# Background work at the joint of two graph-attention layers: read-ahead of second-level sums, late maxima and shifts rearranged

## The chip, the cores and the metric

The kernel runs on one core of one Trainium2 chip. The metric is device time in microseconds (us); lower is better. The core has TensorE (PE in the profile; its weight loads are PEld), VectorE (DVE), ScalarE (ACT), GpSimd (POOL), and 16 DMA engines, whose transfers are issued here from two queues: SyncE's (SP) and POOL's.

## The reference

A graph of N = 2708 nodes with 1024 features goes through two attention layers; `adj` is its 0/1 adjacency matrix. Each layer adds its output to its input.

```python
# layer 0
h = jnp.maximum(_layernorm(x), 0.0)
f = h @ Wf + bf; g = h @ Wg + bg
scores = jnp.where(adj > 0, relu(f @ g.T), NEG)
x = x + softmax(scores, axis=1) @ (h @ W + bW)
# layer 1
h0 = jnp.maximum(_layernorm(x), 0.0)
h = h0 @ W1
e = leaky_relu(h @ a1 + (h @ a2).T, 0.2)
scores = jnp.where(adj > 0, e, NEG)
x = x + relu(softmax(scores, axis=1) @ h)
```

In layer 1 the scores depend on two numbers for each node only, so that its attention weights are made on DVE and ACT. The row maximum that the softmax subtracts follows from the largest second number among a node's neighbours; the code calls these the maxima.

## The kernel before, in words

**Tiles and panels.** The nodes are cut into 22 row tiles: 20 full ones of 128, which go two and two into ten pairs, and two for what is left over (`MONO`, `TINY`). The outputs are made panel by panel: five panels, whose widths are 576, 576, 532, 512 and 512 nodes. The weights of a panel lie transposed: 22 tiles `S[t]`, rows the neighbours, columns the panel's nodes.

**Products.** All large products are in fp32 and use Winograd's form of Strassen's scheme: seven products of half size (M1 to M7) with sums of operands before them and sums of results after them. `aggregate` (L885) makes the features of a panel, normalized h times weights; `project` (L1202) multiplies them by the layer's W. `aggregate` takes its products in the order M1, M5, M2, M6, M3, M7, M4; each runs over ten pairs of tiles and four banks of PSUM (80 matmuls). Product M7 has a point in its middle, after the sixth pair, at which the corner of the left-over tiles is added (`into_m15`, with `gw` banks). In layer 1 panel 0 uses `aggregate`; panels 1 to 4 use `aggregate_quartered` (L1039), in which each of the seven products is cut into seven again. That wants second-level sums of h.

**Second-level sums.** `put_quarters(m, k)` (L392) makes one: it reads the two halves of product m's operand for quad k (two pairs, which are panel k's rows in layer 0) from `hr_d`, does four additions of 128x256 on DVE (tile name `hq`) and stores two halves to `hs2_d`. Reads and stores go through POOL's queue. There are 7 x 5 = 35, seven for each panel, and seven can be made as soon as layer 0 has done that panel's rows.

**Background work.** Work that no product waits for at once is put in lists with a declared cost: `put(us, go, fetch, ..., to)` (L198) appends to `later` (the ordinary list) or to `lazy`. `one` (L201) first issues the reads (`fetch`) of the next `ahead[0]` entries, then does the first entry. `behind(us)` (L211), called at fixed places among the matmuls, grants a credit, and entries of `later` are written out until it is used up; with `spare[0]` set and `later` empty it goes on with `lazy`. `flush` (L218) empties `later`; `exps_until` and `quarters_until` (L416) force what a product needs. `from_slots[0]` decides whether an `hq` tile is taken from the common slots (54 tiles of 128x576) or from the 12 stream buffers. These lists set the order in which the instructions are written; the framework takes that order as a priority and fills idle engines with what is ready, except where `nc.hold` keeps one engine's order.

**Layer 0 to layer 1.** For each panel p layer 0 runs `scores`, the projection of queries for the next panel or, for the last, the projection of panel 3 (L1678 to L1681), and `aggregate`. Panel 4's rows are then projected by pairs of tiles (`by_pair=True`, `rate=0.0`). As row tiles become final, `rows_done` (L1520) adds moments, normalization and dot products to `later`, then the maxima that the new rows bring to panels (`put_max`, L1346: two entries for each panel and pair, one load of a mask through SP and one DVE operation `raise_max`), and second-level sums to `lazy`. For panel 4's two pairs (8 and 9) this is the branch at L1535. Layer 1 has for each panel `shifts1` (L1502: five small transposes of the panel's maxima `mx` on PE, `mx_ps`, L849, and small DVE operations) and `weights1` (L1705: two spreads by PE, L253, then 22 tiles: one ACT operation, two DVE operations, an exponential, and an addition to the running sum `sm`). `take_shifts(p)` (L1781) flushes `later` first. For panel 1 both are hooked into panel 0's aggregate: shifts after M6, weights after M3 (L1794).

```python
        spare[0], from_slots[0] = 0 < p < NP - 1, p == NP - 1        # layer 0, L1688
        G[p] = aggregate(0, p, S, got["sm"], then)
        spare[0] = False
```

So seven sums each of panels 0, 1 and 2 are made in the next panel's aggregate of layer 0, and the fourteen of panels 3 and 4 in layer 1's first one, where `ahead[0]` is 2.

Of the kernel before, what the change touches and what calls it, by code (L numbers as in the profile page):

```python
# [57 lines left out]
def kernel(  # L58
# [26 lines left out]
    NP = N // W  # L85
# [112 lines left out]
    def put(us, go, fetch=None, takes_psum=False, ready=None, to=later):  # L198
        to.append([us, fetch, go, takes_psum, ready])

    def one(of=None):  # L201
        of = later if of is None else of
        for it in of[:ahead[0]]:
            if it[1]:
                it[1]()
                it[1] = None
        us, _, go = of.pop(0)[:3]
        go()
        return us
# [179 lines left out]
    BY_QUARTERS = (M1, M5, M2, M6, M7, M3, M4)  # L389
    made_quarters = {}  # L390

    def put_quarters(m, k):  # L392

        two = []

        def fetch():
            if from_slots[0]:
                two.extend(slot(f"hq{h}", (P, 2, WH)) for h in range(2))
            else:
                t = stream("hq", (P, 4, WH))  # L400
                two.extend(t[:, 2 * h:2 * h + 2] for h in range(2))
            for h in range(2):
                nc.gpsimd.dma_start(two[h], hr_d[:, m, h, :, k])

        def go():
            a11, a12, a21, a22 = (two[h][:, i] for h in range(2) for i in range(2))
            add(a22, a21, a22)
            sub(a21, a11, a21)
            sub(a11, a22, a11)
            sub(a12, a12, a11)  # L410
            for h in range(2):
                store(hs2_d[:, m, 2 * h:2 * h + 2, k], two[h])
            made_quarters[m] = made_quarters.get(m, 0) + 1
        put(1.7, go, fetch, to=lazy)

    def quarters_until(m):  # L416
        while made_quarters.get(m, 0) < NK:
            one(lazy)

    u = consts.tile([P, NC], FP, name="u")  # L420
    v = consts.tile([P, NC], FP, name="v")
# [412 lines left out]
    def load_mask(p, q, k):  # L834
        mt = slot("maskl", (P, WX), BF)
        w = width[p]
        load(mt[:, :w], mk_d[p][:, q, k, :])
        return mt
# [46 lines left out]
    def aggregate(l, p, S, sm, then={}, rate=3.0):  # L885
# [35 lines left out]
        def left_over(ps, e, s, start=False):  # L921


            two = stream("hl", (P, W + 2 * P))
            load(two, hgl_d[l][:, e])
            for d in range(NH):
                nc.tensor.matmul(ps[d], two[:, d * P:(d + 1) * P], S[MONO][:, s], start=start, stop=False,
                                 skip_group_check=True)
            for d in range(NH):
                g = slice(B32 * d, B32 * d + NY)  # L930
                nc.tensor.matmul(ps[d], two[g, W + d % 2 * P:W + (d % 2 + 1) * P], S[TINY][g, s], start=False, stop=start, skip_group_check=True)
# [43 lines left out]
        def scale():  # L975
            for e, s, k in ((0, slice(0, w), w), (1, hi, h)):
# [2 lines left out]
        accumulate(left, right, NQ, h, order, then, evict, "g",  # L979
                   {**prepare, M3: lambda: inverse.append(inverse_sums(p, sm)), M7: scale}, rate=rate,  # L980
                   by_k=True, more={M2: lambda ps: left_over(ps, 0, lo), M3: lambda ps: left_over(ps, 0, hi),
                                    M4: lambda ps: left_over(ps, 1, lo), (M7, NQ // 2): into_m15})
        nc.vector.tensor_tensor(of(1, lo), of(1, lo), by(lo, h), OP.mult)
        return [t.rearrange("p (c i) -> p c i", c=NH) for t in G]

# [357 lines left out]
        t = units[q][k]  # L1343
        nc.vector.scalar_tensor_tensor(mx[p][:n, :w], mk[:n], f[1][:n, t:t + 1], mx[p][:n, :w], op0=OP.add, op1=OP.max)

    def put_max(p, q):  # L1346
        for k in range(2):
            mk = []
            put(0.7, lambda k=k, mk=mk: raise_max(p, q, k, mk[0][:, :width[p]]),
                lambda k=k, mk=mk: mk.append(load_mask(p, q, k)))  # L1350

    def scores(p, B):

# [166 lines left out]
    def rows_done(t, xt):  # L1520

        done_rows[t] = xt

        def dots(k):
            c = t if k else col_of[t]
            dot(f[k][:, c:c + 1], done_rows[t], halves(wab[k]))
            if k == 1:
                nc.vector.tensor_scalar(f2s[:, t:t + 1], f[1][:, t:t + 1], ALPHA, None, op0=OP.mult)
            elif t == MONO:
                nc.gpsimd.dma_start(f[0][:NM, HALF:HALF + 1], f[0][NM:, c:c + 1])  # L1530

        q, k = pair_of.get(t, (LEFT, t - MONO))
        mine = units[q]
        whole = all(s in done_rows for s in mine)
        if panel_of[t] == NP - 1:  # L1535
            done_rows[t] = row_halves("h_last")
            normalize(xt, done_rows[t])
            if whole and q == NQ - 1:
                tc.keep_in_program_order(nc.scalar.activation(stats.tile([P, 1], FP, name="warm"), eps, AF.Exp))
            raise_it = lambda: raise_max(0, q, k, first_mask[t][:, :width[0]])  # L1540
            if not whole:
                dots(1)
                raise_later.append(raise_it)
                put(1.6, lambda: dots(0))
            else:
                raise_later.pop()()
                dots(1)
                raise_it()
                put(1.6, lambda: dots(0))
                rest = []  # L1550
                make = lambda: rest.append(pair_h(q, *(done_rows[s] for s in pairs[q])))
                if q == NQ - 1:
                    got["zm"] = shifts1(0, make)
                else:
                    make()
                rest[0]()
                for p in range(1, NP):
                    put_max(p, q)
                if q == NQ - 1:
                    for m in BY_QUARTERS:  # L1560
                        put_quarters(m, q // 2)
            return

        def met():
            known.add(q)
            for p in range(NP):
                if generated[p] > q:
                    put_max(p, q)
        put(1.5, lambda: moments(xt))
        put(0.5, lambda: normalize(xt))  # L1570
        put(1.6, lambda: dots(0))
        put(1.6, lambda: dots(1))
        if whole and q == LEFT:
            put(0.0, lambda: left_h(1, *(done_rows[s] for s in mine)))
            put(0.0, met)
        elif whole:
            put(2.7, lambda: pair_h(q, *(done_rows[s] for s in pairs[q])))
            put(0.0, met)
            quads_met[q // 2] = quads_met.get(q // 2, 0) + 1
            if quads_met[q // 2] == 2:  # L1580
                put(0.0, lambda: [put_quarters(m, q // 2) for m in BY_QUARTERS])
# [84 lines left out]
    for p in range(NP):  # L1666
        got["S"], got["acc"] = scores(p, B)
        generated[p] = NQ + 1
        ahead[0] = 2
        S = got["S"]  # L1670
        hooks = {M1: lambda p=p: take_max(p), M2: lambda p=p: take_softmax(p)}
        if p == 0:
            hooks[M1] = lambda: (take_max(0), sums_until(3))
            sums_h()
        if p + 1 < NP:
            B = project_q(p + 1, hooks)
        else:
            nc.hold = ("vector",)  # L1678
            project(0, p - 1, G.pop(p - 1), finish0(p - 1), hooks)
            nc.hold = ()  # L1680
            scores_before()  # L1681
        then = {M4: lambda: sums_until(NQ), M5: prepare_W} if p == 0 else {}
        ahead[0] = 1 if p == 0 else 2
        if p == NP - 2:
            then[M2] = lambda: first_masks(NP - 1, 0)
            then[M6] = lambda: first_masks(NP - 1, 1)
            then[M7] = lambda: first_masks(NP - 1, 2)
        spare[0], from_slots[0] = 0 < p < NP - 1, p == NP - 1  # L1688
        G[p] = aggregate(0, p, S, got["sm"], then)
        spare[0] = False  # L1690
        if p == 0:
            flush()
            ahead[0] = 2
            for s in range(1, NP):
                columns_to_row(r_d[s], s, r_[:, first_col[s]:])
            spread_wa()
        if p < NP - 2:
            project(0, p, G.pop(p), finish0(p), {M1: lambda p=p: first_masks(p + 1, 0),
                                                 M5: lambda p=p: first_masks(p + 1, 1),
                                                 M7: lambda p=p: first_masks(p + 1, 2)})  # L1700
# [79 lines left out]

    def take_shifts(p):  # L1781
        flush()
        got["zm"] = shifts1(p)

    def take_weights(p):
# [4 lines left out]
    for p in range(NP):  # L1790
        S, sm = got["P"]
        then = {}
        if p + 1 < NP:
            then = dict(zip((M2, M6) if p else (M6, M3), (lambda p=p: take_shifts(p + 1), lambda p=p: take_weights(p + 1))))  # L1794
        spare[0] = p == 0
        g = aggregate_quartered(p, S, sm, next_right, then, fine=1.0) if p else aggregate(1, p, S, sm, then, rate=4.0)
        hooks = {}
        if p + 1 < NP:
            next_right = quarters_of(p + 1, got["P"][0])
            hooks = {M7: next_right["first"]}  # L1800
        project(1, p, g, finish1(p), hooks, by_pair=(p == NP - 1), rate=1.7)
# [29 lines left out]
```

## Time and profile before

| | us |
|---|---|
| median of 8 runs | 3108.97 (3105.69 to 3111.55) |
| profiled execution, device time | 3109.62 |
| its span | 3107.8 |
| busy in the span: PE, PEld | 3003.0, 2301.9 |
| busy in the span: DVE, POOL, ACT | 2067.8, 505.2, 463.5 |
| mean granted PE clock | 0.986 of full speed |

The joint in PE's timeline (us from the span's start):

| stage | from, to |
|---|---|
| layer 0, aggregate of panel 4 | 1948 to 2080 |
| layer 0, projection of panel 4 by pairs | 2080 to 2129 |
| layer 1, shifts and first weights of panel 0 | 2129 to 2147 |
| layer 1, aggregate of panel 0 | 2147 to 2323 |
| layer 1, projection of panel 0 | 2323 to 2372 |
| layer 1, panel 1 | from 2372 |

How to read it: lines of DVE and ACT carry L45, because a wrapper issues them; operations are told apart by the names of their tiles. `out<-in` names what is written and read, `x14` the count of neighbouring like instructions. In a list of waits the columns are the waiting instruction, what released it, the total, how often and the longest. The device time lies 1.8 us above the span, since it counts what stands around it.

### The profile page before, as it was taken

How to read it: one execution, taken by the hardware profiler on the slowest of the kernel's cores; microseconds unless marked ns; L12 is line 12 of the kernel's file. 1: busy time of each engine (PE TensorE's matmuls, PEld its weight loads, DVE VectorE, ACT ScalarE, POOL GpSimd, SP SyncE). 2: the span in 40 equal slices, each digit the busy share in tenths (PEclk: the TensorE clock that was granted, in tenths of full speed). 3: DMA queues.
4: the chain of work that ended last, by engine and by line, in shares of the span. 5: the costliest groups of instructions: out<-in, count | busy, mean ns of one | idle time of the engine just before them, and what ended most of it. 6: DMA issues, size and time to landing. Idle time of an engine off the chain costs nothing.

```text
span 3107.8 us, 41683 instructions
## 1 busy us (share of the span) xinstructions
PE 3003.0 (97%) x14630; PEld 2301.9 (74%) x14630; DVE 2067.8 (67%) x4615; ACT 463.5 (15%) x817; POOL 505.2 (16%) x786
## 2 busy tenths in 40 slices
PE   8998999899999999999999999998979999999998
PEld 4576777657877588885888886875757969879694
DVE  5776692776751686616974377658787767887853
ACT  3420020000200101101020002203131121312200
POOL 1421101310112110223111101111322011020202
PEclk9999999999999999999999999998989999999999
DMA  6989967998566796668957577587877768878786
GB/s 224 298 256 268 300 245 257 301 277 230 165 239 155 224 251 221 243 157 251 282 189 250 170 219 239 204 278 276 263 235 254 273 197 299 282 271 293 267 294 246
DMA packets 448577, 764.70 MB, mean 246 GB/s; under 512 B 175776, under 2 KB 262592, under 8 KB 448368
## 3 DMA queue, kind: packets, MB, share of 16 engines
q1 hardware_dynamic: 393008, 598.31, 61.1%
q0 software_dynamic: 55360, 163.73, 16.2%
q8 instruction: 116, 1.90, 0.2%
q14 instruction: 93, 0.76, 0.1%
HBM read 627.95 MB, written 133.91 MB: 245 GB/s over the span
## 4 chain that ended last, share of the span: by engine, by line
PE 72%; issue 9%; DVE 9%; DMA 6%; POOL 2%; SPq 2%; ACT 1%; POOLq 0%; DVEq 0%; ACTq 0%
PE sz L1377 6%; PE gx L661 6%; PE gy L661 5%; PE gz L1066 5%; PE gz L661 5%; PE sx L1377 4%; PE pz L1266 4%; PE sy L1377 4%; PE px L1266 4%; PE py L1266 3%; PE gx L1066 3%; PE gy L1066 3%; PE M_ps L574 3%; PE qz L661 3%; PE gv L661 2%
## 5 line engine op out<-in xcount | busy, mean ns | idle before, releaser
L1377 PE MATMUL sz<-B,As 128*128 128x288 f32 (+2 forms) x1200 | 293.6, 394 | 9.5 <-DVE st L45 8.8
L1377 PEld LDWEIGHTS sz<-B,As 128*128 128x128 f32 x1200 | 228.4, 191 | 59.8 <-DVE st L45 12.9
L1377 PE MATMUL sx<-B,As 128*128 128x288 f32 (+2 forms) x800 | 202.1, 396 | 12.8 <-DMA As<-hs_d 11.3
L1377 PE MATMUL sy<-B,As 128*128 128x288 f32 (+2 forms) x800 | 199.0, 392 | 0.0
L661 PE MATMUL gz<-Sa,hc 128*128 128x288 f32 (+2 forms) x800 | 188.3, 396 | 5.8 <-DMA hc<-hg_d 5.8
L1377 PEld LDWEIGHTS sx<-B,As 128*128 128x128 f32 x800 | 152.7, 192 | 46.8 <-DMA As<-hs_d 9.0
L661 PEld LDWEIGHTS gz<-Sa,hc 128*128 128x128 f32 x800 | 153.3, 192 | 39.1 <-DMA hc<-hg_d 6.3
L1377 PEld LDWEIGHTS sy<-B,As 128*128 128x128 f32 x800 | 151.7, 190 | 30.6 <-DVE st L45 0.3
L1066 PE MATMUL gz<-quarter,hc 128*128 128x128 f32 (+2 forms) x1344 | 168.8, 279 | 3.8 <-DVE gT L45 3.7
L143 POOL DMA_DIRECT2D out_dram<-x_res x180 | 88.8, 500 | 479.0 <-DVE x_res L45 472.7
L1066 PEld LDWEIGHTS gz<-quarter,hc 128*128 128x128 f32 x1344 | 160.6, 191 | 5.1 <-DVE gT L45 4.5
L1266 PE MATMUL pz<-w,ps 128*128 128x512 f32 x320 | 142.1, 594 | 0.8 <-DVE pt L45 0.8
L1266 PE MATMUL py<-w,ps 128*128 128x512 f32 x320 | 141.9, 593 | 0.0
L1266 PE MATMUL px<-w,gT 128*128 128x512 f32 x320 | 141.2, 593 | 0.6 <-issue 0.6
L143 POOL DMA_DIRECT2D mk_d<-mask x55 | 35.8, 651 | 531.4 <-DVE mask L45 524.7
L1266 PEld LDWEIGHTS pz<-w,ps 128*128 128x128 f32 x320 | 60.2, 190 | 77.1 <-issue 71.0
L1266 PEld LDWEIGHTS py<-w,ps 128*128 128x128 f32 x320 | 60.6, 190 | 75.5 <-issue 73.1
L574 PE MATMUL M_ps<-wgT,wfT 128*128 128x512 f32 x256 | 112.6, 596 | 1.6 <-ACT hsT L45 1.6
L1266 PEld LDWEIGHTS px<-w,gT 128*128 128x128 f32 x320 | 60.1, 190 | 72.0 <-issue 69.2
L661 PE MATMUL gy<-T,hc 128*128 128x288 f32 (+2 forms) x480 | 111.6, 394 | 0.0
L661 PEld LDWEIGHTS gy<-T,hc 128*128 128x128 f32 x480 | 91.2, 190 | 19.5
L977 POOL TENSOR_TENSOR gT<-gT,rr 128x2304 f32<-128x2304 f32 (+5 forms) x12 | 44.4, 3702 | 372.4 <-issue 158.0
(377 smaller groups left out, 5806.5 us busy)
## 6 DMA issues: line engine op xcount, KB each, us to landing
hc<-hg_d SPq DMA_DIRECT2D x175, 512.0 KB
As<-hs_d SPq DMA_DIRECT2D x150, 512.0 KB
hc<-hr_d SPq DMA_DIRECT2D x119, 512.0 KB
hc<-hs_d SPq DMA_DIRECT2D x112, 512.0 KB
w<-wt_d SPq DMA_DIRECT2D x96, 512.0 KB
w<-in_L_gnn_W_dram SPq DMA_DIRECT2D x72, 512.0 KB
md<-md_d SPq DMA_DIRECT2D x56, 512.0 KB
adj_i<-in_adj_dram SPq DMA_DIRECT2D x200, 128.0 KB
```

The costliest lines, as they stand in the source:

```text
L143: nc.gpsimd.dma_start(a, b)
L574: nc.tensor.matmul(ps, wfT[a][c // NH][:, c % NH, :], wgT[b][c], start=(c == 0), stop=(c == NC - 1))
L661: nc.tensor.matmul(ps[d], left(m, k, d), right(m, k), start=(start and k == 0), stop=(k == K - 1), skip_group_check=True)
L977: nc.gpsimd.tensor_tensor(of(e, s), of(e, s), by(s, k), OP.mult)
L1066: nc.tensor.matmul(ps[:, d], lhs[:, d * P:(d + 1) * P], inner_right(m, n, k), start=(start and k == 0 and d == 0), stop=(k == NK - 1), ski ...
L1266: nc.tensor.matmul(ps, left[i][m][:, k, :], w_[k], start=(start and k == 0), stop=(k == NH - 1), skip_group_check=True)
L1377: nc.tensor.matmul(ps[:n, :h], lefts[q][:, i % 2, c, :n], B[m][c // 2][:, c % 2, :h], start=(start and c == 0), stop=(c == NH - 1), skip_g ...
```

## The change

It has six parts.

1. Entries of `lazy` are read four ahead once `from_slots` is set, and so are those of `later` in layer 1's first aggregate (`ahead[0]` 4 instead of 2; back to 2 after it).
2. The seven sums of panel 4's rows go to `later` instead of `lazy`.
3. Of the maxima that pairs 8 and 9 bring, those of panel 1 stay in `later`; those of panels 2 to 4 go to `lazy`, after the sums. Shifts of panels from 2 on first empty `lazy`.
4. `spare` is also set in layer 0's last aggregate, so that panel 3's seven sums can be made there, and in panel 1 of layer 1.
5. In layer 1's first aggregate the shifts of panel 1 move from behind M6 to behind M3, and its weights from behind M3 into the middle of M7, after the corner.
6. `quarters_until` falls back on `later` when `lazy` is empty.

```diff
     def one(of=None):
         of = later if of is None else of
-        for it in of[:ahead[0]]:
+        for it in of[:4 if of is lazy and from_slots[0] else ahead[0]]:
...
-    def put_quarters(m, k):
+    def put_quarters(m, k, to=lazy):
...
-        put(1.7, go, fetch, to=lazy)
+        put(1.7, go, fetch, to=to)
 
     def quarters_until(m):
         while made_quarters.get(m, 0) < NK:
-            one(lazy)
+            one(lazy if lazy else later)
...
-                                    M4: lambda ps: left_over(ps, 1, lo), (M7, NQ // 2): into_m15})
+                                    M4: lambda ps: left_over(ps, 1, lo),
+                                    (M7, NQ // 2): lambda: (into_m15(), then.get((M7, "middle"), lambda: None)())})
...
-    def put_max(p, q):
+    def put_max(p, q, to=later):
...
-                lambda k=k, mk=mk: mk.append(load_mask(p, q, k)))
+                lambda k=k, mk=mk: mk.append(load_mask(p, q, k)), to=to)
...
-                for p in range(1, NP):
-                    put_max(p, q)
+                put_max(1, q)
                 if q == NQ - 1:
                     for m in BY_QUARTERS:
-                        put_quarters(m, q // 2)
+                        put_quarters(m, q // 2, later)
+                    for p in range(2, NP):
+                        for s in (NQ - 2, NQ - 1):
+                            put_max(p, s, lazy)
...
-        spare[0], from_slots[0] = 0 < p < NP - 1, p == NP - 1
+        spare[0], from_slots[0] = p > 0, p == NP - 1
...
     def take_shifts(p):
         flush()
+        while p > 1 and lazy:
+            one(lazy)
         got["zm"] = shifts1(p)
...
-            then = dict(zip((M2, M6) if p else (M6, M3), (lambda p=p: take_shifts(p + 1), lambda p=p: take_weights(p + 1))))
-        spare[0] = p == 0
+            then = dict(zip((M2, M6) if p else (M3, (M7, "middle")), (lambda p=p: take_shifts(p + 1), lambda p=p: take_weights(p + 1))))
+        spare[0] = p < 2
+        ahead[0] = 2 if p else 4
```

## The prediction

> **What bounds the kernel now.** First the busy times of the page: TensorE (PE) works 3003.0 of 3107.8 us, so only its 105 idle us and its slow-clock time can be won. Then its waits in the stretch that the change touches (1940 to 2520 us): three of its four largest stalls there stand before the maxima of layer 1 (`mx_ps`, L849) and their spreading (L253).
>
> ```profile
> PE mx_ps L849 <- DVE gT L45: 18.8, 1, 18.8
> PE mx_ps L849 <- DVE mx L45: 8.3, 1, 8.3
> PE sp_ps L253 <- DVE m L45: 3.9, 1, 3.9
> PE gv L661 <- DVE m L45: 1.4, 1, 1.4
> ```
>
> PE's timeline places the 18.8: inside product M3 (`gy`) of layer 1's first aggregate. Columns: start, duration, instructions, idle time before and its releaser.
>
> ```profile
> 2229.83 15.68 PE L661 MATMUL gy<-P,hc 128*128 128x288 f32 x64
> ...
> 2248.08 2.21 PE L661 MATMUL gy<-P,hc 128*128 128x288 f32 x8
> 2269.14 1.12 PE L849 MATMUL mx_ps<-ident,mx 128*128 128x128 f32 x4 [18.85 <-DVE gT L45]
> 2270.05 1.17 PE L661 MATMUL gy<-P,hc 128*128 128x288 f32 x2
> 2271.01 0.42 PE L849 MATMUL mx_ps<-ident,mx 128*64 128x128 f32 x1
> 2271.22 3.09 PE L661 MATMUL gy<-P,hc 128*128 128x288 f32 x6
> ```
>
> PE waits for an eviction (`gT<-gy`), which frees a bank for the transposes. VectorE's (DVE) timeline shows why it is late:
>
> ```profile
> 2210.51 2.18 DVE L45 SCALAR_TENSOR_TENSOR mx<-maskl,f,mx 128x512 f32<-128x512 bf16 x3
> 2212.61 0.42 DVE L45 TENSOR_TENSOR hq<-hq 128x256 f32<-128x256 f32 x1
> ...
> 2251.56 0.42 DVE L45 TENSOR_TENSOR hq<-hq 128x256 f32<-128x256 f32 x1 [4.49 <-DMA hq<-hr_d]
> ...
> 2262.49 0.42 DVE L45 TENSOR_TENSOR hq<-hq 128x256 f32<-128x256 f32 x1 [4.68 <-DMA hq<-hr_d]
> ...
> 2268.63 0.81 DVE L45 TENSOR_TENSOR gT<-gy,u 128x288 f32<-128x288 f32 x2
> ```
>
> Fourteen second-level sums (56 `hq` operations, four each) stand in DVE's queue ahead of that eviction, and DVE waits for their reads: from 2212.6 to 2268.7, 4.0 us a sum, of which DVE works 1.7. The maxima were through at 2212.7; it is not they that are late, but what shares the queue. A table of stages (us, PE, PEld, DVE, ACT, POOL, clock, DMA share, GB/s) shows room and lack of room:
>
> ```profile
> 2002.00:2019.00 17.00, 17.00 (x81) 14.96 (x80) 1.86 (x5) 2.37 (x4) 0.00 (x0) 1.00 0.33 116
> 2019.00:2040.00 21.00, 21.00 (x103) 17.98 (x102) 16.08 (x26) 0.00 (x0) 0.00 (x0) 1.00 0.78 273
> 2040.00:2058.00 18.00, 18.00 (x89) 15.34 (x88) 14.11 (x15) 0.00 (x0) 4.83 (x1) 1.00 0.75 257
> 2058.00:2080.00 22.00, 22.00 (x107) 18.85 (x106) 3.87 (x11) 0.00 (x0) 9.03 (x9) 1.00 0.93 217
> 2080.00:2129.00 49.00, 48.22 (x112) 20.81 (x110) 31.91 (x63) 5.75 (x11) 9.22 (x15) 1.00 1.05 383
> 2147.00:2198.00 51.00, 51.00 (x201) 39.60 (x202) 51.00 (x93) 24.77 (x41) 4.32 (x6) 0.95 0.55 170
> 2212.00:2269.00 57.00, 38.29 (x163) 29.19 (x161) 26.62 (x65) 0.00 (x0) 35.55 (x49) 0.87 0.86 288
> ```
>
> In the stall's stage DVE is half idle; in 2147 to 2198 it is full; panel 4's aggregate (to 2080) has DVE and POOL to spare, but DMA fills up towards its end and is full in the projection after it.
>
> [...] clock 0.87 in the stall's stage, and the last 8 `gy` matmuls take 4.26 us where 8 take 1.94 at the pace before (0.2425 each). [...] the `hq` rows show 0.42.
>
> **The change, part by part.** Sums are against the profiled execution: span 3107.8, device time 3109.62, which is 0.65 above the median 3108.97.
>
> *Reads four ahead.* Today the reads of a pair of sums go out, and the next pair's stand in POOL's queue behind stores that wait for DVE: hence 4.0 us a sum. POOL itself needs 2 reads and 2 stores, 4 x 0.73 = 2.9 us; bytes are 4 x 256 KB = 1.05 MB, 3.1 us at the 341 GB/s of the stage's best ten us, other loads apart. Four ahead the pace lies between 2.9 and 4.0; I take 3.3. Eight slots are held instead of four; masks waiting for slots behind them are in SP's queue.
>
> *Panel 3's seven sums.* `spare` now holds in layer 0's panel 4. Do they get a turn there? Its aggregate grants 28 x 3.0 = 84 us of declared cost. Before the sums stand some 10 softmax steps (14), row work of four tiles (4 x 5.2 + 2 x 2.7 = 26.2), eight score steps (14.4) and 20 maxima (14): 68.6. What is left, 15.4, is over seven sums (7 x 1.7 = 11.9): they are written between the middle of M7 and the middle of M4. Their 28 DVE operations (11.9 us) fall into gaps (DVE has 3.9 of 22 us busy at M4), their 28 issues on POOL (20 us) too. Their 7.3 MB are the unknown. At 383 GB/s they take 19 us of all engines; the free shares from 2019 to 2080 are 0.22 x 21 + 0.25 x 18 + 0.07 x 22 = 10.7 us. Some 8 us run into the projection by pairs, whose weights come through SP's queue behind `x_res`, which want slots that the sums now hold. Cost: 0 if the reads start early (DMA is at 0.33 from 2002) or the overflow only delays prefetch; 20 and a slow clock if all of it lands on weights. I take 3. A gain is excluded, as PE has no stall above 0.8 us there.
>
> *Maxima put off.* Of 16 late maxima 12 (panels 2 to 4) leave the path: 12 x 0.73 = 8.7 us of DVE, and 12 loads on SP. DVE thus comes to the first sum at about 2204 instead of 2212.6. The seven sums of panel 4 (now in the ordinary queue, which the flush empties) end near 2204 + 7 x 3.3 = 2227, before the next eviction (`u<-gz`, PE ready 2230). The 12 maxima then fit between 2230 and 2250, where only 1.8 us of evictions fall. If their masks come late they hold up `gT<-gy` a little: 0 to 5, taken as 1.
>
> *Shifts after M3, weights in the middle of M7.* Shifts move 20 us later; their bank is then free in any case. So the 18.85 goes, with the slow clock after it: 4.26 - 1.94 = 2.3 for `gy`, 0.8 for the transposes (1.54 against 0.77 in the next panel), 0.4 for `sum_ps` (1.49 against 1.13). The 1.4 before `gv` goes too, since M7's corner eviction now stands ahead of the weights. Sum: 23.7. Against it: weights now start about 10 us into M7 (24 matmuls 5.8, corner 2.9, spreading 1.3) instead of 3.6 (2275.4 to 2279.0), 6.5 later against PE. They are 22 steps of 2.5 us on DVE (22.9 + 16.4 + 15.7 = 55); the last ended at 2349.8 and panel 1's quarters began at 2366.0, so 16 us of slack hide the 6.5. If that slack is not there, it costs 6.5. DVE is busier in the projection; 1 us for that. Queued behind the weights on DVE are the projection's evictions, for which PE would wait.
>
> *No effect:* the fallback in `quarters_until` and the loop ahead of later shifts find nothing left to do. The 8.3 and 3.9 at layer 1's start are a chain of small operations that is not touched.
>
> **Sum:** -23.7 + 3 + 1 + 1 = -18.7; 3109.6 - 18.7 = 3090.9, less 0.65 for the median: 3090.
>
> **Rivals.** *The stall shrinks only in part* (3098, chance 0.15). The 57 us of the stall's stage already move 288 GB/s; if seven sums stay in layer 1's lazy queue, DMA limits them however far ahead they are read. 14 x 3.3 = 46 us from 2204 end at 2250, and with slot waits of masks (SP's waits show 10.1 us for one on `hs_d<-hq`) half of 23.7 stays. Against it: the tally of 68.6 in 84. *No change that can be measured* (3109, chance 0.12): what is saved in layer 1 is paid at the projection by pairs. *Slower by over 6 us* (3118, chance 0.21): panel 3's sums get slots only when M7 ends (2060) and stand in DVE's in-order queue ahead of `gT<-gv` and the `ps` sums, which have under 1 us of slack (`ps` ready 2082.5, PE there at 2083.2). With DMA at 0.93 and 1.05 a sum then takes 6 to 8 us instead of 4; seven end at 2102 to 2116, and PE waits 20 to 33 us plus 3 of slow clock: 32 - 23.7 = +8. It decides from a pace of about 6 us a sum, if they start at 2060. For it: slots are full there (SP waits up to 16.7 us on DVE `P`). Against it: sums of panels 0 to 2 already run in such aggregates without a stall of PE, and POOL can read ahead.
>
> **Numbers.** Likeliest, the stall gone with small new costs: 0.52, 3084 to 3096. About 0.2% (6 us) is what a measurement of this kernel can tell from no change. Faster 0.67 (the first two cases), same 0.12, slower 0.21. The range runs from 3084 (23.7 won and a little of the start) to 3114, leaving out about 5 in 100 below and 15 above.
>
> **What would show it.** Right: no wait of `mx_ps` on `gT`; 28 of the 56 slot `hq` operations of DVE before 2085, 28 in layer 1 at under 3.6 us a sum; the clock of the stall's stage back near 1.0; `gv` without a wait. Wrong: PE waits in the projection by pairs (`px`, `py`, `pz` on `w`, `x_res` or `ps`), 56 `hq` operations still in layer 1, or a new wait of `gz<-quarter` at the head of panel 1.

## The result, and the profile after

The changed kernel takes 3096.44 us (median of 10 runs, 3094.58 to 3102.83) against 3108.24 for the kernel before (28 runs beside it): a ratio of 0.9964, 95% interval 0.9956 to 0.9972. The medians differ by 11.8 us. Its profiled execution took 3100.43 us, with a span of 3098.6 us.

TensorE (PE) does the same work in a shorter span; its idle time fell from 104.8 to 93.7 us. The page of the changed kernel:

```profile
span 3098.6 us, 41680 instructions
PE 3004.9 (97%) x14630; PEld 2301.9 (74%) x14630; DVE 2070.2 (67%) x4615; ACT 463.2 (15%) x817; POOL 505.4 (16%) x786
```

The joint is measured from PE's timeline, between instructions that every version has: the first product of layer 0's last aggregate, the first of its projection by pairs, the first of layer 1's first aggregate, of its projection, and of panel 1. One profiled execution of each:

| us | aggregate of panel 4 | projection by pairs, start of layer 1 | layer 1, aggregate of panel 0 | its projection | joint |
|---|---|---|---|---|---|
| before | 132.10 | 66.95 | 176.48 | 48.87 | 424.40 |
| after | 133.84 | 75.59 | 152.59 | 50.31 | 412.33 |
| difference | +1.74 | +8.64 | -23.89 | +1.44 | -12.07 |

The gain lies in layer 1's aggregate of panel 0. The projection by pairs has a loss that takes a third of it. Behind the joint the two executions need the same (735.71 and 735.63 us); ahead of it the one of after was 2.95 us slower, in a stretch that the change doesn't touch.

PE's waits in the stretch that the prediction used (1940 to 2520 us), after: the 18.8 of the transposes on `gT` is gone, and a wait of the projection for its weights has come. The 2.2 us on `V`, in panel 1, stood there before too; the prediction's list left them out.

```profile
PE mx_ps L849 <- DVE mx L45: 8.3, 1, 8.3
PE px L1267 <- DMA w<-in_L_gnn_W_dram: 5.8, 1, 5.8
PE sp_ps L253 <- DVE m L45: 4.4, 2, 3.9
PE gz L1082 <- DVE V L45: 2.2, 1, 2.2
PE px L1267 <- ACT pt L45: 1.5, 1, 1.5
PE gv L661 <- DVE m L45: 1.2, 1, 1.2
```

PE's timeline where the stall stood, after. No line has an idle time in brackets, and 16 `gy` matmuls take 4.15 us:

```profile
2260.53 4.15 PE L661 MATMUL gy<-P,hc 128*128 128x288 f32 x16
2264.52 1.13 PE L864 MATMUL sum_ps<-sm,ones 128*128 128x288 f32 x4
2265.49 0.71 PE L849 MATMUL mx_ps<-ident,mx 128*128 128x128 f32 x5
2266.03 11.81 PE L661 MATMUL gz<-P,hc 128*128 128x288 f32 x48
```

VectorE (DVE) after: panel 3's sums lie in layer 0 (first and last `hq` lines), panel 4's in layer 1, and now it is DVE that waits for PE before the eviction `gT<-gy`.

```profile
2055.96 0.43 DVE L45 TENSOR_TENSOR hq<-hq 128x256 f32<-128x256 f32 x1 [0.71 <-DMA hq<-hr_d]
...
2078.80 0.42 DVE L45 TENSOR_TENSOR hq<-hq 128x256 f32<-128x256 f32 x1
...
2215.68 0.42 DVE L45 TENSOR_TENSOR hq<-hq 128x256 f32<-128x256 f32 x1
...
2236.45 0.42 DVE L45 TENSOR_TENSOR hq<-hq 128x256 f32<-128x256 f32 x1
...
2261.81 0.46 DVE L45 TENSOR_TENSOR gT<-gy,u 128x288 f32<-128x288 f32 x1 [16.81 <-PE gy L661]
```

The loss, in PE's timeline of after: the second `px` product of the projection by pairs waits 5.80 us for weights and then runs at a granted clock of 0.61 (6.14 us; 3.60 where the clock is 1.00). 5.80 + 2.54 = 8.3 of the 8.64.

```profile
2097.31 6.14 PE L1267 MATMUL px<-w,gT 128*128 128x512 f32 x8 [5.80 <-DMA w<-in_L_gnn_W_dram]
```

The weights are asked for late. In SP's queue they stand behind the 32 loads of `x_res`, whose issue took 20.4 us before (from 2054.06) and takes 30.3 after (from 2057.23). Counted from the start of the aggregate, the weights are asked for 10.1 us later. Before, then after:

```profile
2074.57 1.68 SPq L139 DMA_DIRECT2D w<-in_L_gnn_W_dram  x2
```

```profile
2087.61 1.50 SPq L139 DMA_DIRECT2D w<-in_L_gnn_W_dram  x2
```

The table of windows of after shows the load behind this. The columns are as in the prediction's table. The DMA engines are full (share 1 or more) from the end of the aggregate to the end of the projection. Before, the last 22 us of the aggregate were at a share of 0.93 and moved 217 GB/s; now 352.

```profile
2061.00:2084.00 23.00, 21.77 (x104) 18.06 (x103) 16.28 (x38) 0.00 (x0) 17.23 (x22) 1.00 1.02 352
2084.00:2142.00 58.00, 51.42 (x115) 21.92 (x114) 32.16 (x64) 5.43 (x10) 13.23 (x19) 0.94 1.05 353
```

### The profile page after: what moved, and what is told of

Same layout as the page of the kernel before. It is cut to its first block, busy times and chain, and to the rows that moved or that the text cites. A ratio compares the mean times of both kernels' runs of the same rounds, so it can differ in the third digit from the quotient of the medians.

```text
span 3098.6 us, 41680 instructions
## 1 busy us (share of the span) xinstructions
PE 3004.9 (97%) x14630; PEld 2301.9 (74%) x14630; DVE 2070.2 (67%) x4615; ACT 463.2 (15%) x817; POOL 505.4 (16%) x786
## 4 chain that ended last, share of the span: by engine, by line
PE 72%; DVE 11%; DMA 7%; issue 7%; POOL 1%; ACT 1%; SPq 1%; POOLq 0%; DVEq 0%; ACTq 0%
PE sz L1378 7%; PE gx L661 6%; PE gy L661 6%; PE gz L661 5%; PE gz L1067 5%; PE sy L1378 4%; PE sx L1378 4%; PE px L1267 4%; PE pz L1267 3%; PE gx L1067 3%; PE M_ps L574 3%; PE gy L1067 3%; PE py L1267 3%; PE gv L661 2%; PE qz L661 2%
```

## The experiments

Theory: the stall went because only half as many sums stand ahead of the eviction (part 4), and the price is their traffic at the projection by pairs. Rivals: the hooks that were moved (part 5) or the reads four ahead (part 1) removed the stall; and for the price, slots or the order of SP's queue instead of bytes. Sizes are those of the table above. The two executions of the same changed kernel (after and e5_again) differ by 0.7 us in the joint; and in the column of layer 1's aggregate its first product alone differs by up to 1.5 us (20.68 us in e3_no_spare, 22.22 before at a granted clock of 0.88, 21.34 after at 0.92). Part 3 (late maxima), part 2 and part 6 were not run alone.

| run | aggregate of panel 4 | projection, start | layer 1, panel 0 | its projection | joint | ratio to before, 95% |
|---|---|---|---|---|---|---|
| e1_spare_only | 133.29 | 79.56 | 153.27 | 48.86 | 414.98 | 0.9954 (0.9941 to 0.9966) |
| e2_hooks_only | 132.11 | 66.93 | 175.98 | 51.73 | 426.75 | 1.0002 (0.9992 to 1.0012) |
| e3_no_spare | 132.11 | 66.94 | 171.16 | 50.23 | 420.44 | 0.9983 (0.9972 to 0.9994) |
| e4_traffic_only | 132.11 | 81.27 | 176.35 | 48.86 | 438.59 | 1.0020 (1.0012 to 1.0028) |
| e5_again | 133.68 | 75.95 | 153.12 | 50.31 | 413.06 | 0.9959 (0.9944 to 0.9974) |
| e6_two_ahead | 133.69 | 78.49 | 153.22 | 51.75 | 417.15 | 0.9978 (0.9970 to 0.9986) |
| e7_w_first | 134.08 | 78.71 | 153.05 | 50.30 | 416.14 | 0.9972 (0.9964 to 0.9980) |
| e8_spare_w_first | 133.52 | 81.37 | 154.09 | 48.87 | 417.85 | 0.9977 (0.9970 to 0.9984) |
| e9_hooks_back | 133.85 | 75.65 | 157.54 | 48.07 | 415.11 | 0.9976 (0.9968 to 0.9983) |
| e10_four_early | 133.98 | 68.96 | 158.92 | 50.25 | 412.11 | 0.9966 (0.9954 to 0.9978) |
| e11_two_early | 132.10 | 66.96 | 166.21 | 50.25 | 415.52 | 0.9970 (0.9959 to 0.9981) |
| e12_three_early_hooks_back | 133.75 | 66.99 | 167.28 | 48.07 | 416.09 | 0.9968 (0.9955 to 0.9981) |

### Part 4 alone

The kernel before with one line of the change. The other half of part 4, `spare` in panel 1 of layer 1, is not in it.

```diff
-        spare[0], from_slots[0] = 0 < p < NP - 1, p == NP - 1
+        spare[0], from_slots[0] = p > 0, p == NP - 1
```

> The kernel before with part 4 alone: panel 3's seven sums may run in layer 0's last aggregate, reads two ahead, hooks and maxima as before. Theory (the stall is the length of DVE's queue of sums, and the price is the sums' traffic at the joint): layer 1 keeps seven sums, which end near 2212 + 7 x 4.0 = 2240, so the 18.8 us wait of mx_ps on gT goes with its slow clock (-22); the projection by pairs pays about as in the changed kernel (+8 to +10): net -12 to -14, near 3096. Rival (the place of the shifts is what removes the stall): with the shifts still behind M6 the mx_ps wait stays above 10 us, and the time is 3100 to 3118.

The theory held: the first aggregate of layer 1 fell by 23.2 us, almost as in the full change, with two sums read ahead, the maxima in their old place and the hooks where they were. The price appears too, larger by 4.0 us and with other names in PE's list of waits:

```profile
PE pz L1266 <- DVE pt L45: 6.2, 1, 6.2
...
PE py L1266 <- DMA w<-in_L_gnn_W_dram: 1.9, 1, 1.9
```

By time this line alone can't be told from the whole change: the intervals of its ratio (0.9941 to 0.9966) and of the changed kernel's (0.9956 to 0.9972) overlap.

### Part 5 alone

The kernel before with the two hooks moved.

```diff
-                                    M4: lambda ps: left_over(ps, 1, lo), (M7, NQ // 2): into_m15})
+                                    M4: lambda ps: left_over(ps, 1, lo),
+                                    (M7, NQ // 2): lambda: (into_m15(), then.get((M7, "middle"), lambda: None)())})
...
-            then = dict(zip((M2, M6) if p else (M6, M3), (lambda p=p: take_shifts(p + 1), lambda p=p: take_weights(p + 1))))
+            then = dict(zip((M2, M6) if p else (M3, (M7, "middle")), (lambda p=p: take_shifts(p + 1), lambda p=p: take_weights(p + 1))))
```

> The kernel before with part 5 alone: shifts behind M3, weights in the middle of M7; all fourteen sums in layer 1, two ahead. Theory (queue of sums): DVE comes to gT<-gy no earlier than before, some 38 us after M6 ends; PE no longer stops for mx_ps, does the first half of M7 (12 us) meanwhile and then waits for banks of the corner (gw) or of the sums' row (sum_ps) for 5 to 10 us: a gain of 9 to 14, 3094 to 3099, and no wait at the projection. Rival (the place of the shifts alone makes the stall): all 23.7 are won, 3085.

Both were wrong: nothing was won. The stall kept its releaser and changed the instruction that bears it, since what PE wants next after M3 waits for the same late eviction:

```profile
PE sum_ps L864 <- DVE gT L45: 21.4, 1, 21.4
```

So moving the waiting instruction behind the product does not help while the eviction is late. The projection of panel 0 grew by 2.9 us, with the weights later.

### All but part 4

The changed kernel with the line of e1_spare_only turned back: fourteen sums in layer 1, read four ahead.

> The changed kernel without part 4: panel 3's sums stay in layer 1's first aggregate, behind panel 4's, four ahead; the projection by pairs is as before the change. Theory: the 10.4 us that the changed kernel pays between panel 4's aggregate and layer 1 come back (no wait of px on w, none of gv on m). What is paid instead is what fourteen sums at 3.3 us leave of the stall: they end near 2204 + 46 = 2250 in the old time scale, with the maxima 2259, against the eviction at 2250, so 0 to 9 us of wait around M3 or the corner. Time 3086 to 3096. Rival (DMA limits fourteen sums however far ahead): half of the 23.7 stays, 3098 or more.

The price at the projection by pairs goes entirely, as forecast (66.94 us). But only 5.3 of the 23.9 us are won: the rival's side, though not for its reason. PE now waits for `hc`, and SP's queue shows that these loads were not slow but not issued: one wait of 36.7 us, on the store of a sum, whose slot a mask load wanted.

```profile
PE gy L661 <- DMA hc<-hr_d: 11.9, 2, 6.1
```

```profile
SPq L139 <- DMA hs_d<-hq: 57.9, 11, 36.7
```

```profile
2168.39 15.88 SPq L139 DMA_DIRECT2D hc<-hr_d  x5
2221.10 3.26 SPq L139 DMA_DIRECT2D maskl<-mk_d  x2
```

SP issues nothing from 2184.3 to 2221.1, and the window inside that gap moves 37 GB/s at a DMA share of 0.10:

```profile
2192.00:2212.00 20.00, 20.00 (x88) 15.20 (x87) 19.93 (x43) 3.93 (x8) 2.28 (x4) 1.00 0.10 37
```

Eight slots of sums read ahead are held until DVE, busy with softmax weights (19.93 us in that window of 20), comes to them; the mask load waits for one, and every `hc` load behind it waits too. That is read from SP's wait; it is not the whole account. The changed kernel also reads eight halves ahead there, and SP's longest wait is then 11.7 us (on DVE's `P`). Why the block is so much longer with fourteen sums, and whether two ahead would avoid it, was not run alone.

### The traffic alone

The kernel before with 28 stores of 256 KB on POOL's queue, issued in the last aggregate of layer 0, where part 4 adds its sums. They write features into rows of the output that the kernel overwrites later, and use no slot, no DVE and no read.

```diff
                 nc.gpsimd.tensor_tensor(of(e, s), of(e, s), by(s, k), OP.mult)
+            for i in range(28 if l == 0 and p == NP - 1 else 0):
+                nc.gpsimd.dma_start(out[i % 14 * P:(i % 14 + 1) * P, i // 14 * W:(i // 14 + 1) * W], of(0, slice(0, W))[:, i % NH])
```

> The kernel before with 28 more stores of 256 KB on POOL's queue (7.3 MB, the bytes of panel 3's sums) between the two scalings of panel 4's aggregate: rows of the output are written with features that are overwritten later by the real output. No slot is held and no DVE operation is added. Theory A (bandwidth: the traffic slows x_res and with it the weights behind it in SP's queue): PE waits 4 to 9 us for w in the projection by pairs and the time rises by 6 to 11, to 3114 to 3119. Theory B (slots: x_res waits for slots that the sums hold): no such wait, time within 2 us of before, 3107 to 3110.

The same 7.3 MB without sums bring the wait of `px` on weights, and 14.3 us in the projection of this execution, the slowest of its fifteen (6.2 us by the ratio, 3.7 to 8.7):

```profile
PE px L1268 <- DMA w<-in_L_gnn_W_dram: 8.1, 1, 8.1
```

So this traffic suffices for the price; slots and DVE's order are not needed. By which queue the stores delay the weights is not shown for this run; in after the same weights come through SP's queue (asked for at 2087.61).

### Two ahead, and weights first

The changed kernel was run once more beside these, as a yardstick.

> The changed kernel once more, on the same chip as the three beside it. Ratio to before 0.996 to 0.997, a wait of px on w of 4 to 8 us in the projection by pairs.

It repeated its joint within 0.7 us. e6_two_ahead is the changed kernel without part 1:

```diff
-        for it in of[:4 if of is lazy and from_slots[0] else ahead[0]]:
+        for it in of[:ahead[0]]:
...
-        ahead[0] = 2 if p else 4
```

> The changed kernel without part 1: reads two ahead everywhere. Theory (what counts is how many sums stand in layer 1's queue, not how far ahead they are read): layer 1 has seven sums at 4.0 us, which end by 2240 in the old time scale, before the eviction at 2250; its stage is as in the changed kernel within 1 us, the time within 3 us of it. Rival (the read-ahead is what shortens the queue): a wait of sum_ps or mx_ps on gT of 5 us or more comes back, 5 to 10 us slower than the changed kernel.

The stall does not come back (153.22 against 153.12), as the theory said; the joint is 4.1 us longer, where it allowed 3. What reading ahead is worth lies in the projections: 2.5 us by pairs, 1.4 in that of panel 0. e7_w_first asks for the third product's weights ahead of `x_res` in SP's queue, in the changed kernel; e8_spare_w_first does it with part 4 alone.

```diff
-        ws = {m: load_W(l, m) for m in order[:2]}
+        ws = {m: load_W(l, m) for m in order[:3 if by_pair and l == 0 else 2]}
```

> The changed kernel with the weights of the projection's third product (M2) asked for ahead of x_res in SP's queue instead of behind its 32 loads. Theory (the collision costs because the traffic slows x_res, behind which w stands in SP's queue): the 5.8 us wait of px on w goes with 2.5 us of slow clock; x_res comes 2 to 3 us later, for which DVE and not PE waits: 3 to 8 us faster than the changed kernel. Rival (plain bandwidth: all bytes are needed by then): a wait of the same length shows at another product (py or pz on w or pt), time within 2 us of the changed kernel.

> The kernel before with two edits only: part 4 (panel 3's sums in layer 0's last aggregate) and the weights of M2 ahead of x_res. Theory (part 4 is all that the change gains; parts 1, 2, 3 and 5 give nothing together): as fast as the changed kernel with w first, within 3 us. Rival (the other parts gain too): slower than that by 4 us or more.

The theory of SP's order fell in both: e8_spare_w_first's projection takes 1.8 us more than e1_spare_only's. In e7_w_first `px` no longer waits, but the next weights do, and the projection takes 2.8 us more than in e5_again, not less:

```profile
PE pz L1267 <- DMA w<-wt_d: 5.4, 1, 5.4
...
PE py L1267 <- DMA w<-in_L_gnn_W_dram: 2.4, 1, 2.4
```

Asking for one load earlier made another late; in after the DMA share of this stretch was 1.05. The forecast for e8_spare_w_first itself held: its joint is within 3 us of e7_w_first's (417.85 and 416.14).

### Part 5 undone

The changed kernel with the two edits of e2_hooks_only turned back.

> The changed kernel with part 5 undone: the shifts of panel 1 behind M6 and its weights behind M3, as before the change. Theory (the gain of layer 1's first aggregate comes from part 4 alone, part 5 only delays the weights): the first aggregate stays at 153 us, no wait of the transposes on gT, and the projection after it falls from 50.3 to 48.9 us, so 1 to 2 us faster than the changed kernel in the profile and a ratio to the kernel before of about 0.9955. Rival (part 5 is needed because the flush in take_shifts now comes earlier with seven sums still in it): the stall returns in part, 3 to 8 us, with mx_ps waiting on gT or mx behind hq operations, and a ratio of 0.997 or more.

The transposes wait for nothing, so that the stall is not part 5's to remove; its projection is 2.2 us shorter, as the theory said. But the aggregate is 4.4 us longer than in e5_again, by the rival's amount and another wait: the corner's evictions (`m<-gw`) stand behind some eight steps of panel 1's weights on DVE, and `gv` waits 2.81 us for their bank and then runs slower (17.48 us for 64; 15.68 in after, where the granted clock was 1.00).

```profile
2292.84 1.55 DVE L45 TENSOR_TENSOR m<-gw,m 128x288 f32<-128x288 f32 x4
```

```profile
2293.35 17.48 PE L661 MATMUL gv<-P,hc 128*128 128x288 f32 x64 [2.81 <-DVE m L45]
```

Net, part 5 is worth 2 to 3 us of the changed kernel's joint. It depends on the other parts: in e1_spare_only, whose hooks stand in the old place too, `gv` waits only 1.45 us and runs in 15.79, as before the change. Why it waits longer here is not shown.

### How many sums early

The changed kernel, in which only some of panel 3's seven sums are made in layer 0's last aggregate and `keep` of them stay for layer 1. `keep` is 3 in e10_four_early, 5 in e11_two_early, and 4 in e12_three_early_hooks_back, which also undoes part 5.

```diff
-        for it in of[:4 if of is lazy and from_slots[0] else ahead[0]]:
+        for it in of[:max(1, min(4, len(of) - keep[0])) if of is lazy and from_slots[0] else ahead[0]]:
...
-        while spare[0] and not later and lazy and credit[0] > 0:
+        while spare[0] and not later and len(lazy) > keep[0] and credit[0] > 0:
...
+        keep[0] = 3 if p == NP - 1 else 0
         G[p] = aggregate(0, p, S, got["sm"], then)
+        keep[0] = 0
```

> The changed kernel, but only four of panel 3's seven sums are made in layer 0's last aggregate; three stay for layer 1's first one. A test of dose. Theory (the collision's price goes with the bytes that meet the projection by pairs): with 4/7 of the 7.3 MB the price of 10.4 us in aggregate and projection of panel 4 falls to about 6 (projection 72 instead of 75.6). In layer 1 three more sums at 3.0 us fill 9 of the 16.8 us in which DVE idled before gT, so the first aggregate stays within 1 us of 153 and the joint is about 4 us shorter than the changed kernel's 412 to 413: ratio to the kernel before 0.9945. Rival (the price is a threshold, paid as soon as any sums are in flight at the hand-over): projection stays at 74 to 76, ratio 0.996. Second rival (late sums delay gT again): first aggregate 158 or more.

> As the run with four sums early, but with two early and five left for layer 1. Theory: the collision's price falls to 2/7 of 10.4, about 3 us (projection 69 to 70), and five more sums at 3.0 us take 15 of DVE's 16.8 idle us before gT, so that the first aggregate is still near 153 but at its edge, 153 to 156: the joint is 5 to 7 us shorter than the changed kernel's, ratio to the kernel before 0.994. Rival (the stores of twelve sums hold slots and masks wait in SP's queue, as with fourteen): the first aggregate is 160 to 168, and the joint no shorter than the changed kernel's, ratio 0.996 to 0.998, with PE waiting on hc<-hr_d or on gT.

> Three of panel 3's sums early, four left, and part 5 undone: shifts behind M6 and weights behind M3 as before the change. If dose and hooks are independent: projection of panel 4 near 71, first aggregate 153, projection of panel 0 48.9, so that the joint is about 405 to 407 us against 412 to 413 of the changed kernel and 424 before it: ratio 0.9935 to 0.994, better than both. Rival (with the earlier shifts the four late sums stand again in DVE's queue ahead of the eviction that the transposes wait for): a wait of mx_ps or sum_ps on gT of 5 to 12 us comes back, first aggregate 158 to 165, ratio 0.996 or more.

Over the projection by pairs the dose is not a straight line but a knee: 66.95, 66.96, 66.99, 68.96 and 75.6 to 76.0 us for 0, 2, 3, 4 and 7 sums early. The aggregate ahead of it takes 132.1 us with 0 and 2, and 133.7 to 134.0 with 3, 4 and 7. In layer 1 the theory was wrong: DVE's 16.8 idle us are not free room. With 7, 10, 12 and 14 sums left for it (all read four ahead, hooks moved) its first aggregate takes 153, 158.9, 166.2 and 171.2 us. The eviction is not late; PE waits for `hc`, and SP's queue is blocked, as the rival of e11_two_early had it. SP's longest wait grows with the sums that are left: 11.7 us with 7, 28.7 with 10 (both put down to DVE's `P`), 32.7 with 12 and 36.7 with 14 (both to the store of a sum). In e12_three_early_hooks_back, with 11 left, it is 26.5, on DVE's `hq`, and its forecast of 153 us was missed by 14. In e11_two_early PE's wait, SP's, and a window inside SP's (17 GB/s at a DMA share of 0.05):

```profile
PE gy L662 <- DMA hc<-hr_d: 7.3, 1, 7.3
```

```profile
SPq L139 <- DMA hs_d<-hq: 54.6, 11, 32.7
```

```profile
2195.00:2212.00 17.00, 17.00 (x76) 12.87 (x75) 16.93 (x39) 1.97 (x4) 2.13 (x3) 1.00 0.05 17
```

What four early save in layer 0 (7.0 us against e5_again) they lose in layer 1 (5.8); the joint, 412.1, is that of the changed kernel. No version here beats it by more than the intervals allow.

## Why the prediction was right or wrong

**The stall (-23.7): its size right, its cause only in part.** Measured -23.89 in that stage, with the clock (1.00), the transposes and `gv` back at their usual pace. That the two agree within 0.2 is partly chance: 0.9 of it is the first product, which the sum did not contain. And the prediction let the gain come from four parts together. Part 4 alone gives 23.2 of it; "Shifts move 20 us later; their bank is then free in any case. So the 18.85 goes" is refuted by e2_hooks_only, where the stall only takes the name `sum_ps`. That the bank is free depends on the eviction, and that on the sums ahead of it.

**Reads four ahead.** The pace was near the estimate of 3.3: seven sums in 23.3 us in layer 0 (3.3), in 21.2 in layer 1 (3.0). It was not what removed the stall (e6_two_ahead). With fourteen sums the rest of the change put a new one in its place (e3_no_spare); the held slots, which the prediction mentioned without a price, have a part in it.

**The turn for panel 3's sums.** The tally of 68.6 in 84 us came out: first reads at 2051.2, all 28 operations between 2056.0 and 2079.2.

**The collision (+3): the term that was mis-sized.** It measured +8.64 in the projection, and +1.74 in the aggregate, of which 1.2 are `gv` waiting behind `hq` for the corner's evictions: 10.4 in place of 3. What failed is the choice of 3 itself: that the overflow would mostly delay prefetch. The prediction's own table had the projection at a share of 1.05, so that nothing there was left to delay, and the cost came out as 5.8 us of waiting and 2.5 of slower running at the granted clock of 0.61.

The step before it, "Some 8 us run into the projection by pairs", agrees with these 8.3 in part by luck. It sets 19 us of traffic against 10.7 us of free DMA shares from 2019 on. But the first read goes out 100.5 us into the aggregate, where the prediction's tally had put it; that is 2048.2 in the time of before. From there the same shares leave 0.25 x 10 + 0.07 x 22 = 4.0 us, the traffic of 1.5 sums. Yet three early sums cost the projection nothing, and four 2.0 us. By the 10.7 the knee would lie at 3.9 sums, but 6.6 of them come before the sums can start; so why the knee lies where it does stays open.

**Maxima put off (+1).** No delay of `gT<-gy`: DVE waited 16.8 us for PE before it.

**Weights later (+1).** +1.44 in the projection of panel 0, and e9_hooks_back takes it away. The kind of wait is the predicted one, evictions that queue behind the weights, but mostly on another engine: `px` waits 1.51 us for ACT's copy of `pt`, and a `pz` 0.23 for DVE's. In the changed kernel it is worth more that the corner's evictions stand ahead of the weights (e9_hooks_back: 2.81 and 1.8).

**The sum.** -18.7 predicted, -12.07 in the joint of the profile and -11.8 in the medians. The difference, 6.6, is the collision (7.4 too little) less what the other terms gave. The time alone would not have chosen the case: 3096.44 lies just above the likeliest one (3084 to 3096) and close to the first rival's 3098. The traces choose it: every sign of being right came (no wait of `mx_ps` on `gT`, 28 operations in each layer at 3.3 and 3.0 us a sum, the clock, `gv` in layer 1). But so did one sign of being wrong, `px` waiting on `w`.

**The rivals.** The slower one had the right place and the wrong mechanism: a sum took 3.3 us, not 6, and `gT<-gv` waited for PE, never for a sum; the weights were what came late. Of the rival "the stall shrinks only in part", e3_no_spare showed the time but not the reason (a blocked queue at a DMA share of 0.10, not a full one).

## What to carry to other kernels

When work is moved out of one stage into another, look at the DMA share of the receiving stage and of the one behind it, and only from the moment at which the moved work can start. Where both were full after the change here (shares of 1.02 and 1.05), the added traffic came out as waiting at a load that PE needed (5.8 us), with a product at a granted clock of 0.61 behind it (2.5 us). Here a stall on a late buffer stayed with the queue that frees it: moving the waiting instruction only renamed it (18.8 us on `mx_ps` before, 21.4 on `sum_ps` in e2_hooks_only). In e3_no_spare buffers that were read ahead had a part in blocking loads of quite another kind, through one entry that waited 36.7 us in an issuing queue, while the DMA engines were nearly idle (a share of 0.10); look at what the queue's head waits for before a wait for a load is put down to bandwidth.

## What the runs showed of the hardware

An addition of 128x5 that took 0.15 us in e9_hooks_back, where it ran before POOL's scaling of features (2265.17 against 2270.34), took 4.30 in the changed kernel, and ended with that scaling (2269.15 + 5.05 = 2274.20; DVE's 2274.23). DVE's and POOL's timelines of after:

```profile
2269.93 4.30 DVE L45 TENSOR_TENSOR z<-f,mcol 128x5 f32<-128x5 f32 x1
```

```profile
2269.15 5.05 POOL L977 TENSOR_TENSOR gT<-gT,rr 128x2304 f32<-128x2304 f32 x1 [31.26 <-DVE rr L45]
```

The two overlap for 4.27 of the 4.30 us and end within 0.03 us of each other; what held the addition up, the trace does not show. It cost PE nothing here: the spreading of its result starts at 2281.01.
